# Weight sums kept in DRAM, transposes in other PSUM banks and 512-column value products in a four-layer hybrid network

## The chip, the cores and the metric

The kernel runs on one core of one Trainium2 chip. The metric is the device time of one execution in microseconds, from its first to its last instruction with what the device adds around them; the median of the runs is quoted.

## The reference

`x` is [4, 512, 256] in f32. Four layers are applied, each as `x = x + layer(layernorm(x))`: full attention (16 heads of 128), a gated linear layer, a low-rank attention, and the gated layer again with the same weights. The change touches only the first layer and the norms:

```
q = einsum('bpd,hde->bphe', x, W_Q) + b_Q          # k and v the same with W_K, W_V
scores = einsum('bqhe,bkhe->bhqk', q, k) / sqrt(128), causal
z = einsum('bkhe,bhqk->bqhe', v, softmax(scores))
out = einsum('bqhe,hed->bqd', z, W_O) + b_O
```

The weights do not depend on the batch, so each of the four batches projects with the same ones.

## The kernel before, in words

`attention_full` runs 64 units (4 batches of 16 heads), one per call of `step(i)`, for i = 0 to 64. The order of instructions on each engine is the order in which the code issues them (a manual schedule), and each engine works through its own list without overtaking. Step i holds several units at different ages:

- scores, softmax and `divide` of unit i: four score matmuls of 128 to 512 columns (L468), a masked maximum on VectorE (L476), exponentials on ScalarE (L479), a reciprocal (L491) and the division on GpSimd (L494);
- `turn` of unit i-1 in four pieces (32x32 transposes on VectorE, L503) and `carry(i-1)`: SyncE writes the result to DRAM (`way`, L514), waits for it, and reads it back in four pieces as `probsT` (L517);
- `mix(i-2)`: probabilities times values (L530) and the output products (L552) of a group of four units;
- the query and key projections of unit i+1, and a part of the value projection of the next group.

**The projections are made with seven products instead of eight.** Query and key of a head are taken together as one product of 2x2 blocks; weights and positions are combined first, then seven block products (L395) give the four blocks. `combine_weights` makes three sums s1, s2, s4 and overwrites one block (a21) with a difference: four GpSimd instructions (L306 to L309), of 128 columns for a head (`combine_head`) and of 256 for a group's values (`combine_values`). `combine_positions` makes the like for the positions of a batch (L296 to L299), on GpSimd for batches 1 to 3. The returned list `a11, a12, s4, a22, s1, s2, a21` is indexed by the product's number less one: product 1 uses a11, 2 uses a12, 6 uses s2, 7 uses a21, 5 uses s1, 3 uses s4. In the page the sums are called `extra` (even heads) and `extra_w` (odd heads), the sums of positions `extra_x`.

The order inside `step(i)` matters for all that follows. Product 1 of unit i+1 stands first, then scores 0 and 1, the first `turn`, products 2 and 6, score 2, one value product, product 7, score 3, `divide`, the last turns, `carry(i-1)`, products 5 and 4, `load(i)`, `mix(i-2)`, product 3, `combine_head(i+2)`, and outputs. Between them stand pieces of other layers (`beside`, from a table written by hand).

The sums of unit i+2 are made in step i, and product 6 of step i+1 is the first to read them. SyncE issues every DMA: in a step `way`, four `probsT`, then `load(i)`: for odd i the weights wk and wq of a later pair of heads (L253), for i = 2 mod 4 the values' weights wv (L258), for i = 0 mod 4 the output weights wo (L263).

PSUM has eight banks of 512 columns: three `ps_sc`, two `ps_tp`, two `ps_mm`, one `ps_pz`. Query and key products and the transposes of the norms (L223) and of the gated layer (L1041) use `ps_tp`. A group's value projection (`project_group`) is done in two rounds of seven products of 256 columns, one position tile each time, accumulated in `ps_sc` and `ps_mm` and copied out by ScalarE (L410) and VectorE (L406).

Of the kernel before, what the change touches and what calls it, by code (L numbers as in the profile page):

```python
# [11 lines left out]
F32 = mybir.dt.float32  # L12
# [11 lines left out]
H = 16  # L24
# [42 lines left out]
def network(ctx: ExitStack, tc: tile.TileContext, ins: dict, out: bass.AP):  # L67
# [22 lines left out]

    def ps_pz():
        return psum.tile([P, 512], F32, tag="pz", name="ps_pz")


    ctx.enter_context(tc.manual_schedule())
# [91 lines left out]
    def norm(b, take, extra=None, tiles=range(NT), xT=None, short=False):  # L187


        stats = lnpool.tile([P, NT, 6], F32, name="stats")  # L190
        mv = lnpool.tile([P, NT, 2], F32, name="mv")
        for t in tiles:
            nc.vector.bn_stats(stats[:, t, :], x[b][t])
            nc.vector.bn_aggr(mv[:, t, :], stats[:, t, :])
            yield
        rstd = lnpool.tile([P, NT], F32, name="rstd")
        shift = lnpool.tile([P, NT], F32, name="shift")
        some = slice(tiles[0], tiles[-1] + 1)
        nc.gpsimd.tensor_scalar(rstd[:, some], mv[:, some, 1], EPS, None, ALU.add)
        nc.gpsimd.tensor_tensor(rstd[:, some], rstd[:, some], minus_half[:, some], ALU.pow)  # L200
        if not short:
            nc.gpsimd.tensor_tensor(shift[:, some], mv[:, some, 0], rstd[:, some], ALU.mult)
            nc.gpsimd.tensor_scalar(shift[:, some], shift[:, some], -1.0, 1.0, ALU.mult, ALU.mult)
        yield
        yield
        xT = xT or new_xT()

        def normalise(t):
            xn = lnpool.tile([P, D], F32, name="xn")
            if short:  # L210
                nc.vector.tensor_scalar(
                    xn, x[b][t], mv[:, t, 0:1], rstd[:, t : t + 1], ALU.subtract, ALU.mult
                )
            else:
                nc.scalar.activation(
                    xn, x[b][t], AF.Identity, bias=shift[:, t : t + 1], scale=rstd[:, t : t + 1]
                )
            return xn

        def transpose(t, xn):  # L220
            pt = ps_tp()
            for c in range(DC):
                nc.tensor.transpose(pt[:, c * P : (c + 1) * P], xn[:, c * P : (c + 1) * P], ident)  # L223
# [19 lines left out]
    def attention_full(events, prologue):  # L243
# [2 lines left out]
        n = len(units)  # L246
        wq, wk, wv, wo = {}, {}, {}, {}

        def load_pair(p, w):
            h = 2 * p % H  # L250
            name = "wq" if w is wq else "wk"
            w[p] = slot(f"{name}{p % 2}", name).rearrange("p (c n) -> p c n", c=DC)
            nc.sync.dma_start(w[p], ins["a_" + name][:, :, h * DH : (h + 2) * DH])  # L253

        def load_values(g):
            h = HG * g % H
            wv[g] = slot(f"wv{g % 2}", "wv").rearrange("p (c n) -> p c n", c=DC)
            nc.sync.dma_start(wv[g], ins["a_wv"][:, :, h * DH : (h + HG) * DH])  # L258

        def load_output(g):  # L260
            h = HG * g % H
# [29 lines left out]
        def combine_positions(b, engine):  # L291
# [4 lines left out]
            engine.tensor_tensor(t3, b22, b12, ALU.subtract)  # L296
            engine.tensor_tensor(b12, b12, b11, ALU.subtract)
            engine.tensor_tensor(t2, b22, b12, ALU.subtract)
            engine.tensor_tensor(t4, b21, t2, ALU.subtract)  # L299
            moving[b] = b11, b21, b22, t4, b12, t2, t3  # L300

        def combine_weights(a11, a12, a21, a22, place):

            cols = a11.shape[-1]
            s1, s2, s4 = (place[:, i * cols : (i + 1) * cols] for i in range(3))
            nc.gpsimd.tensor_tensor(s1, a21, a22, ALU.add)  # L306
            nc.gpsimd.tensor_tensor(a21, a11, a21, ALU.subtract)
            nc.gpsimd.tensor_tensor(s2, s1, a11, ALU.subtract)
            nc.gpsimd.tensor_tensor(s4, a12, s2, ALU.subtract)  # L309
            return a11, a12, s4, a22, s1, s2, a21  # L310

        def keep(b):
            def take(xT):
                xTs[b] = xT
                if b:
                    combine_positions(b, nc.gpsimd)

            return take

# [53 lines left out]

        stationary, open_sums = {}, {}

        def combine_head(u):

            p, j = divmod(u, 2)
            (a11, a12), (a21, a22) = (
                [w[p][:, c, j * DH : (j + 1) * DH] for c in range(DC)] for w in (wq, wk)  # L380
            )
            place = extra[2] if j else extra[0][:, 3 * S :]
            stationary[u] = combine_weights(a11, a12, a21, a22, place)

        def combine_values(g):

            a11, a21, a12, a22 = (
                wv[g][:, c, i * HD : (i + 1) * HD] for c in range(DC) for i in range(2)
            )
            stationary["v", g] = combine_weights(a11, a12, a21, a22, extra[0][:, g % 2 * 3 * HD :])  # L390

        def product(i, ps, weights, positions, of_values, start):
            a, b = weights[i - 1], positions[i - 1]
            lhsT, rhs = (b, a) if of_values else (a, b)
            nc.tensor.matmul(  # L395
                ps[:, :HS], lhsT=lhsT, rhs=rhs, start=start, stop=True, skip_group_check=True
            )

        def seven(u, places, biases, positions, chain, side):

            of_values = isinstance(u, tuple)
            weights = stationary[u[:2]] if of_values else stationary[u]
            c11, c12, c21, c22 = places

            def onto(ps, place):
                nc.vector.tensor_tensor(place, place, ps[:, :HS], ALU.add)  # L406

            def out(ps, place, bias):
                if bias is None:
                    nc.scalar.copy(place, ps[:, :HS])  # L410
                else:
                    nc.scalar.activation(place, ps[:, :HS], AF.Identity, bias=bias)  # L412

            def on_chain(i, place, bias):
                if i == 1:
                    open_sums[u, "x"] = chain()
                ps = open_sums[u, "x"]
                product(i, ps, weights, positions, of_values, i == 1)
                out(ps, place, bias)

            def on_side(i, place):
                if i != 3:
                    open_sums[u, "z"] = side()
                ps = open_sums[u, "z"]
                product(i, ps, weights, positions, of_values, i != 3)
                onto(ps, place)

            return {
                1: lambda: on_chain(1, c11, biases[0]),
# [8 lines left out]
        def project(u):  # L438
# [6 lines left out]
            return seven(u, places, biases, moving[b], ps_tp, ps_tp)  # L445

        def project_group(g, t):

            b = HG * g // H
            if t == 0:  # L450
                values[g] = slot(f"v{g % 2}", "v").rearrange("p (t n) -> p t n", t=NT)
            places = [
                values[g][:, t + 2 * i, j * HD : (j + 1) * HD] for j in range(2) for i in range(2)
            ]
            positions = [a[:, t * P : (t + 1) * P] for a in moving[b]]
            return seven(("v", g, t), places, (None, None), positions, ps_sc, ps_mm)

        def score(u, t):

# [121 lines left out]
            project_plainly(u, wk)  # L581
        for t in range(2, NT):
            project_values(0, t)
        combine_positions(0, nc.vector)
        take_bias(0)()
        combine_head(2)
        of_group = {}

        def step(i):
            b, h = divmod(i, H)  # L590
# [148 lines left out]
    def gated(layer, l, xT, xT_before, half, after, last=False):  # L739
# [298 lines left out]
        pt = ps_tp()[:, : nt * DC * P]  # L1038
        for i in range(nt):
            for c in range(DC):  # L1040
                nc.tensor.transpose(  # L1041
# [126 lines left out]
    def attention_lowrank(xTs, events):  # L1168
# [254 lines left out]
        def prologue(i):  # L1423
# [8 lines left out]
            elif stage == -2:  # L1432
                load_keys()
            elif stage == 0:
                buffers()
                probs_of(0, [split(f"squares{k}", k) for k in range(2)])
                probs_of(3, [slot("probs1", "probs3")])
# [291 lines left out]
```

## Time and profile before

| what | value |
|---|---|
| three runs | 1380.65, 1383.38, 1385.46 us (median 1383.38) |
| profiled execution, own time | 1385.7 us |
| its span, first to last instruction | 1383.8 us |
| mean granted TensorE clock | 0.982 |
| TensorE matmul busy | 1286.0 us (93%) |
| VectorE, ScalarE, GpSimd busy | 856.4, 690.2, 729.6 us |
| full attention, first score to last L552 | about 27 to 835 us |
| batches 2 and 3 of it | about 387 to 800 us |

A busy engine need not be at its peak, and a share over the whole span mixes four layers. The chain of waits and the timeline of one step tell what sets the end. In the timeline a row reads: start, duration, engine, line, operation, output<-inputs, shape, count, and in brackets the idle time before it with what ended it. "SPq" is SyncE issuing a DMA; a PE row of "x2" is one f32 matmul, which the profile records as two passes.

### The profile page before, as it was taken

Reading aid. Unit: us, or ns where it says so; the run is one execution under the profiler, and the core shown is the slowest. Engines: PE = TensorE matmul, PEld = TensorE weight load, DVE = VectorE, ACT = ScalarE, POOL = GpSimd, SP = SyncE. Lnnn points to the kernel's source line nnn. Section 1 sums busy time; section 2 is a strip of 40 time slices with the busy share of each in tenths; the row PEclk is TensorE's granted clock in tenths of the full one; section 3 lists DMA queues with packets and bytes.
Section 4 is the critical chain, followed back from the end, with each engine's and each line's share of the span. In section 5 each row is a group of like instructions: output and inputs, shape, how many; then the busy total and the mean of one; then the engine's idle time right before and its main releaser. Section 6 shows DMA issues by size and latency. Waiting matters only on the chain.

```text
span 1383.8 us, 19620 instructions
## 1 busy us (share of the span) xinstructions
PE 1286.0 (93%) x5774; PEld 899.4 (65%) x5774; DVE 856.4 (62%) x2614; ACT 690.2 (50%) x1960; POOL 729.6 (53%) x1433
## 2 busy tenths in 40 slices
PE   8899999999998999899989888998999999999996
PEld 5677776777776777677767565545655676655554
DVE  4566555664775665775746855695566655575756
ACT  3534444454443444343444336655666665767641
POOL 4544443652448344573436655676564765765660
PEclk9999999999999999999999999999999999999998
DMA  3667775555555353454643530000000000000000
GB/s 95 209 202 215 224 196 193 160 160 156 154 166 149 118 160 126 141 164 129 181 117 111 150 107 16 1 1 1 1 1 9 9 9 1 9 1 8 1 9 16
DMA packets 88154, 133.97 MB, mean 97 GB/s; under 512 B 16112, under 2 KB 69872, under 8 KB 88048
## 3 DMA queue, kind: packets, MB, share of 16 engines
q1 hardware_dynamic: 88048, 132.72, 32.3%
q8 instruction: 47, 0.77, 0.2%
q14 instruction: 59, 0.48, 0.1%
HBM read 86.29 MB, written 46.40 MB: 96 GB/s over the span
## 4 chain that ended last, share of the span: by engine, by line
PE 69%; DVE 12%; POOL 8%; ACT 5%; issue 3%; DMA 2%; SPq 1%; DVEq 0%; POOLq 0%; ACTq 0%
PE ps_tp L395 10%; PE ps_sc L468 8%; PE ps_pz L530 8%; PE ps_mm L552 7%; PE ps_mm L781 6%; PE ps_sc L1339 6%; PE ps_tp L1375 4%; PE ps_pz L1395 4%; PE ps_sc L395 3%; PE ps_mm L1413 3%; PE ps_mm L960 2%; PE ps_mm L395 2%; PE ps_mm L1313 1%; POOL probs L1367 1%; DMA probsT<-way 1%
## 5 line engine op out<-in xcount | busy, mean ns | idle before, releaser
L494 POOL TENSOR_SCALAR probs<-probs,sums 128x128 f32<-128x128 f32 (+3 forms) x256 | 137.0, 553 | 368.2 <-DVE sums L491 363.1
L479 ACT ACTIVATE probs<-ps_sc,sums 128x128 f32<-128x128 f32 (+3 forms) x256 | 134.7, 527 | 129.5 <-DVE sums L476 124.9
L468 PE MATMUL ps_sc<-kT,qT 128*128 128x128 f32 (+3 forms) x512 | 172.4, 440 | 10.3 <-ACT probs L479 10.3
L1367 POOL TENSOR_SCALAR probs<-probs,sums 128x160 f32<-128x160 f32 (+3 forms) x224 | 120.4, 555 | 108.4 <-DVE sums L1364 84.8
L476 DVE CUSTOM_DVE_ANT_0 ps_sc<-ps_sc,mask_a 128x128 f32<-128x128 f32 (+3 forms) x256 | 126.8, 500 | 81.2 <-PE ps_sc L468 65.2
L1347 DVE CUSTOM_DVE_ANT_0 ps_sc<-ps_sc,mask_b 128x96 f32<-128x96 f32 (+15 forms) x256 | 112.0, 448 | 94.2 <-PE ps_sc L1339 81.3
L1350 ACT ACTIVATE probs<-ps_sc,sums 128x160 f32<-128x160 f32 (+3 forms) x224 | 114.1, 512 | 99.7 <-DVE sums L1347 78.0
L412 ACT ACTIVATE qT<-ps_tp,bias 128x256 f32<-128x256 f32 x124 | 58.2, 469 | 209.9 <-PE ps_tp L395 209.9
L1339 PE MATMUL ps_sc<-kTb,qTb 128*128 128x32 f32 (+15 forms) x512 | 156.2, 414 | 5.5 <-ACT probs L1350 5.4
L530 PE MATMUL ps_pz<-probsT,v 128*128 128x512 f32 (+3 forms) x512 | 149.2, 434 | 7.0 <-DMA probsT<-way 6.1
L530 PEld LDWEIGHTS ps_pz<-probsT,v 128*128 128x128 f32 x512 | 96.4, 190 | 64.9 <-issue 35.7
L552 PE MATMUL ps_mm<-wo,zT 128*128 128x256 f32 x512 | 123.7, 386 | 1.4 <-ACT qTb L1247 1.3
L503 DVE STREAM_TRANSPOSE squares<-probs 128x512 f32<-128x512 f32 (+3 forms) x256 | 120.6, 491 | 0.0
L1380 ACT COPY probsT<-ps_tp 128x512 f32<-128x512 f32 x160 | 92.2, 585 | 40.5 <-PE ps_tp L1375 39.0
L552 PEld LDWEIGHTS ps_mm<-wo,zT 128*128 128x128 f32 x512 | 97.7, 193 | 17.1 <-ACT qTb L1247 1.7
L1375 PEld LDWEIGHTS ps_tp<-ident,probs 128*128 128x128 f32 x608 | 71.6, 143 | 51.5 <-issue 27.8
L468 PEld LDWEIGHTS ps_sc<-kT,qT 128*128 128x128 f32 x512 | 86.8, 193 | 25.5 <-ACT probs L479 13.9
L1375 PE MATMUL ps_tp<-ident,probs 128*128 128x128 f32 x608 | 96.5, 283 | 4.7 <-ACT xT L225 1.5
L1339 PEld LDWEIGHTS ps_sc<-kTb,qTb 128*128 128x128 f32 x512 | 82.5, 196 | 24.4 <-ACT probs L1350 9.9
L781 PE MATMUL ps_mm<-w_in,cx 128*128 128x512 f32 (+1 forms) x256 | 91.7, 496 | 2.6 <-DVE cx L766 1.1
L543 DVE TENSOR_SCALAR zT<-ps_pz,bias 128x512 f32<-128x512 f32 x64 | 47.9, 748 | 66.9 <-PE ps_pz L530 66.9
L395 PE MATMUL ps_tp<-extra_x,wk 128*128 128x256 f32 x248 | 75.4, 386 | 3.6 <-ACT qT L412 3.5
(215 smaller groups left out, 2616.5 us busy)
## 6 DMA issues: line engine op xcount, KB each, us to landing
way<-squares SPq DMA_DIRECT2D x64, 640.0 KB, 2.9
probsT<-way SPq DMA_DIRECT2D x256, 160.0 KB, 3.3
wv<-in_a_wv_dram SPq DMA_DIRECT2D x16, 512.0 KB, 5.1
wq<-in_a_wq_dram SPq DMA_DIRECT2D x32, 256.0 KB, 4.0
wk<-in_a_wk_dram SPq DMA_DIRECT2D x32, 256.0 KB, 3.9
wo<-in_a_wo_dram SPq DMA_DIRECT2D x16, 512.0 KB, 4.7
x<-in_x_dram SPq DMA_DIRECT2D x16, 128.0 KB, 3.8
out_dram<-x SPq DMA_DIRECT2D x16, 128.0 KB, 1.7
```

The lines of the kernel that those rows point to most:

```text
L395: nc.tensor.matmul(ps[:, :HS], lhsT=lhsT, rhs=rhs, start=start, stop=True, skip_group_check=True)
L468: nc.tensor.matmul(ps[:, :m], lhsT=queries[u][:, t * P : (t + 1) * P], rhs=keys[u][:, :m], start=True, stop=True,)
L476: nc.vector.tensor_tensor_reduce(ps[:, :m], ps[:, :m], mask[:, S - m :], -scale, 3.0e38, ALU.add, ALU.min, nmax[:, t : t + 1])
L479: nc.scalar.activation(pr[:, t, :m], ps[:, :m], AF.Exp, bias=nmax[:, t : t + 1], scale=-1.0, accum_out=total[:, t : t + 1],)
L494: nc.gpsimd.tensor_scalar(pr[:, t, :m], pr[:, t, :m], inv[:, t : t + 1], 1.0, ALU.mult, ALU.mult)
L503: nc.vector.transpose(squares[u].rearrange("p (j n b) -> p n j b", j=NQ, b=Q)[:, f : f + m], probs[u][0][:, k:, k * P : (k + 1) * P].rearr ...
L530: nc.tensor.matmul(z[:, :, k:, :], lhsT=v[:, k, j * DH : (j + 1) * DH], rhs=pT[:, :, f : f + m, :], start=(k == 0), stop=(k == NT - 1),)
L552: nc.tensor.matmul(po[:, :D], lhsT=zTs[HG * g + i][:, t].rearrange("p i b -> p (i b)"), rhs=wo[g][:, i, :], start=(i == 0), stop=(i == HG ...
L781: nc.tensor.matmul(ps[:, : hi - lo], lhsT=cx[:, c, i * P : (i + 1) * P], rhs=w_in[:, c, lo:hi], start=(c == 0), stop=(c == DC - 1),)
L1339: nc.tensor.matmul(ps, lhsT=q[:, t % 2 * 4 + i].rearrange("p h q -> p (h q)"), rhs=kT[:, :m], start=True, stop=True,)
L1367: nc.gpsimd.tensor_scalar(probs[i][:, :m], probs[i][:, :m], inv[:, i : i + 1], 1.0, ALU.mult, ALU.mult)
L1375: nc.tensor.transpose(pt.rearrange("p (h i q) -> p h i q", h=4, i=4)[:, :, i, :], lw["probs"][t][s][i][:, k * P : (k + 1) * P], ident,)
```

## The change

Four edits.

1. **Weight sums kept.** From batch 1 on, the sums of each head and group and the overwritten wk and wv are stored to DRAM (`keep_head`, `keep_values`). In batches 2 and 3 `combine_head` and `combine_values` issue a load from there in place of the four GpSimd instructions, and wk and wv are loaded as they were stored.
2. **Positions.** `combine_positions` is done on VectorE for every batch, in steps 8 and 9 of the batch before, two instructions each.
3. **Transposes** of the norms and of the gated layer use `ps_mm` during full attention, and `ps_tp` afterwards.
4. **Values.** A group's value projection is one round over four steps; each product is two matmuls of 256 columns into the two halves of a bank, and one copy of 512 columns.

In the first batch `combine_head(2)` is also issued ahead of the addition of the output bias. The core of the diff:

```
+        kept = {}
+        def keep_or_load(what, place):
+            if what not in kept:
+                kept[what] = dram.tile([P, place.shape[-1]], F32, name="kept_%s%d" % what)
+                nc.sync.dma_start(kept[what], place)
+            else:
+                nc.sync.dma_start(place, kept[what])
...
-            w[p] = slot(f"{name}{p % 2}", name).rearrange("p (c n) -> p c n", c=DC)
-            nc.sync.dma_start(w[p], ins["a_" + name][:, :, h * DH : (h + 2) * DH])
+            flat = slot(f"{name}{p % 2}", name)
+            w[p] = flat.rearrange("p (c n) -> p c n", c=DC)
+            if w is wk and ("k", h) in kept:
+                keep_or_load(("k", h), flat)
+            else:
+                nc.sync.dma_start(w[p], ins["a_" + name][:, :, h * DH : (h + 2) * DH])
...
-            nc.gpsimd.tensor_tensor(s1, a21, a22, ALU.add)
-            nc.gpsimd.tensor_tensor(a21, a11, a21, ALU.subtract)
-            nc.gpsimd.tensor_tensor(s2, s1, a11, ALU.subtract)
-            nc.gpsimd.tensor_tensor(s4, a12, s2, ALU.subtract)
+            if not known:
+                nc.gpsimd.tensor_tensor(s1, a21, a22, ALU.add)
+                nc.gpsimd.tensor_tensor(a21, a11, a21, ALU.subtract)
+                nc.gpsimd.tensor_tensor(s2, s1, a11, ALU.subtract)
+                nc.gpsimd.tensor_tensor(s4, a12, s2, ALU.subtract)
...
-            place = extra[2] if j else extra[0][:, 3 * S :]
-            stationary[u] = combine_weights(a11, a12, a21, a22, place)
+            known = ("h", u % H) in kept
+            if known:
+                keep_or_load(("h", u % H), extra_of_head(u))
+            stationary[u] = combine_weights(a11, a12, a21, a22, extra_of_head(u), known)
+
+        def keep_head(u):
+            if u >= H and ("h", u % H) not in kept:
+                keep_or_load(("h", u % H), extra_of_head(u))
+            if u >= H and u % 2 and ("k", u % H - 1) not in kept:
+                keep_or_load(("k", u % H - 1), wk[u // 2].rearrange("p c n -> p (c n)"))
...
-            pt = ps_tp()
+            pt = for_transposes[0]()
...
+            def products(w, i):
+                return [(t, moving[b][i][:, t * P : (t + 1) * P], w) for t in range(2)]
+            return seven(("v", g), stationary["v", g], places, (None, None), products, ps_sc, ps_mm)
...
-                if j % 2 == 0:
-                    of_group.update(project_group(g + 1, j // 2))
-                group = [(1,), (2, 6), (), ()] if j % 2 == 0 else [(7,), (5,), (4,), (3,)]
+                if j == 0:
+                    of_group.update(project_group(g + 1))
+                group = [
+                    [(1,), (), (2,), ()],
+                    [(6,), (), (), ()],
+                    [(7,), (5,), (), ()],
+                    [(4,), (3,), (), ()],
+                ][j]
...
+            if b + 1 < B and 8 <= h < 10:
+                next(of_positions.setdefault(b + 1, combine_positions(b + 1)))
...
             of_head(5, 4)
+            if 2 <= i + 1 < n:
+                keep_head(i + 1)
+            if i % HG == 1 and i // HG + 1 < groups:
+                keep_values(i // HG + 1)
             load(i)
```

`combine_values` and `keep_values` are the same for a group's sums ("e", 768 columns) and wv ("v", 1024 columns). In the built order the list of SyncE grows from 529 to 601 instructions: 32 stores (16 of a head's sums, 8 of a pair's wk, 4 and 4 for the values) and 40 loads of sums (32 of a head, 8 of a group) are added, and 24 loads of wk and wv change their source. A head's sums are 128 x 384 f32, 192 KB.

More of the change, by code (lines that the diff above doesn't have):

```diff
@@ L92, in ps_pz @@
         return psum.tile([P, 512], F32, tag="pz", name="ps_pz")
+    for_transposes = [ps_mm]
     ctx.enter_context(tc.manual_schedule())
@@ L251, in load_pair @@
             name = "wq" if w is wq else "wk"
-            w[p] = slot(f"{name}{p % 2}", name).rearrange("p (c n) -> p c n", c=DC)
-            nc.sync.dma_start(w[p], ins["a_" + name][:, :, h * DH : (h + 2) * DH])
+            flat = slot(f"{name}{p % 2}", name)
[4 more added lines that the diff above has]
+                nc.sync.dma_start(w[p], ins["a_" + name][:, :, h * DH : (h + 2) * DH])
         def load_values(g):
             h = HG * g % H
-            wv[g] = slot(f"wv{g % 2}", "wv").rearrange("p (c n) -> p c n", c=DC)
-            nc.sync.dma_start(wv[g], ins["a_wv"][:, :, h * DH : (h + HG) * DH])
+            flat = slot(f"wv{g % 2}", "wv")
+            wv[g] = flat.rearrange("p (c n) -> p c n", c=DC)
+            if ("v", h) in kept:
+                keep_or_load(("v", h), flat)
+            else:
+                nc.sync.dma_start(wv[g], ins["a_wv"][:, :, h * DH : (h + HG) * DH])
         def load_output(g):
@@ L289, in attention_full, with combine_positions @@
         HS, HD = S // 2, HG // 2 * DH
-        def combine_positions(b, engine):
+        def combine_positions(b):
             b11, b12, b21, b22 = (xTs[b][:, c, i * HS : (i + 1) * HS] for c in range(DC) for i in range(2))
@@ L295, in combine_positions, with combine_weights @@
             t2, t3, t4 = (of_batch[:, i * HS : (i + 1) * HS] for i in range(3))
[L296 to L299, printed above, removed]
             moving[b] = b11, b21, b22, t4, b12, t2, t3
-        def combine_weights(a11, a12, a21, a22, place):
+            nc.vector.tensor_tensor(t3, b22, b12, ALU.subtract)
+            nc.vector.tensor_tensor(b12, b12, b11, ALU.subtract)
+            yield
+            nc.vector.tensor_tensor(t2, b22, b12, ALU.subtract)
+            nc.vector.tensor_tensor(t4, b21, t2, ALU.subtract)
+            yield
+        def combine_weights(a11, a12, a21, a22, place, known):
             cols = a11.shape[-1]
             s1, s2, s4 = (place[:, i * cols : (i + 1) * cols] for i in range(3))
-            nc.gpsimd.tensor_tensor(s1, a21, a22, ALU.add)
-            nc.gpsimd.tensor_tensor(a21, a11, a21, ALU.subtract)
-            nc.gpsimd.tensor_tensor(s2, s1, a11, ALU.subtract)
-            nc.gpsimd.tensor_tensor(s4, a12, s2, ALU.subtract)
+            if not known:
[3 more added lines that the diff above has]
+                nc.gpsimd.tensor_tensor(s4, a12, s2, ALU.subtract)
             return a11, a12, s4, a22, s1, s2, a21
@@ L314, in take @@
                 xTs[b] = xT
-                if b:
-                    combine_positions(b, nc.gpsimd)
             return take
@@ L374, in attention_full, with extra_of_head, extra_of_group @@
         stationary, open_sums = {}, {}
+        def extra_of_head(u):
+            return (extra[2] if u % 2 else extra[0][:, 3 * S :])[:, : 3 * DH]
+        def extra_of_group(g):
+            return extra[0][:, g % 2 * 3 * HD :][:, : 3 * HD]
         def combine_head(u):
@@ L389, in combine_values, with keep_values, seven, multiply @@
             )
[L390 to L402, printed above, removed]
-            c11, c12, c21, c22 = places
[L405 to L412, printed above, removed]
+            known = ("e", HG * g % H) in kept
+            if known:
+                keep_or_load(("e", HG * g % H), extra_of_group(g))
+            stationary["v", g] = combine_weights(a11, a12, a21, a22, extra_of_group(g), known)
+        def keep_values(g):
+            if HG * g >= H and ("e", HG * g % H) not in kept:
+                keep_or_load(("e", HG * g % H), extra_of_group(g))
+                keep_or_load(("v", HG * g % H), wv[g].rearrange("p c n -> p (c n)"))
+        def seven(u, weights, places, biases, products, chain, side):
+            c11, c12, c21, c22 = places
+            def multiply(i, ps, start):
+                for at, lhsT, rhs in products(weights[i - 1], i - 1):
+                    nc.tensor.matmul(
+                        ps[:, at * HS : (at + 1) * HS],
+                        lhsT=lhsT,
+                        rhs=rhs,
+                        start=start and at == 0,
+                        stop=True,
+                        skip_group_check=True,
+                    )
+            def like(ps, place):
+                cols = math.prod(place.shape[1:])
+                ps = ps[:, :cols]
+                return ps if len(place.shape) == 2 else ps.rearrange("p (t n) -> p t n", t=place.shape[1])
             def on_chain(i, place, bias):
@@ L417, in on_chain @@
                 ps = open_sums[u, "x"]
-                product(i, ps, weights, positions, of_values, i == 1)
-                out(ps, place, bias)
+                multiply(i, ps, i == 1)
+                if bias is None:
+                    nc.scalar.copy(place, like(ps, place))
+                else:
+                    nc.scalar.activation(place, like(ps, place), AF.Identity, bias=bias)
             def on_side(i, place):
@@ L424, in on_side @@
                 ps = open_sums[u, "z"]
-                product(i, ps, weights, positions, of_values, i != 3)
-                onto(ps, place)
+                multiply(i, ps, i != 3)
+                nc.vector.tensor_tensor(place, place, like(ps, place), ALU.add)
             return {
@@ L444, in project, with project_group, products @@
             biases = [bias[:, i, h : h + 1] for i in range(2)]
-            return seven(u, places, biases, moving[b], ps_tp, ps_tp)
-        def project_group(g, t):
+            def products(w, i):
+                return [(0, w, moving[b][i])]
+            return seven(u, stationary[u], places, biases, products, ps_tp, ps_tp)
+        def project_group(g):
             b = HG * g // H
-            if t == 0:
-                values[g] = slot(f"v{g % 2}", "v").rearrange("p (t n) -> p t n", t=NT)
+            values[g] = slot(f"v{g % 2}", "v").rearrange("p (t n) -> p t n", t=NT)
             places = [
-                values[g][:, t + 2 * i, j * HD : (j + 1) * HD] for j in range(2) for i in range(2)
+                values[g][:, 2 * i : 2 * i + 2, j * HD : (j + 1) * HD] for j in range(2) for i in range(2)
             ]
-            positions = [a[:, t * P : (t + 1) * P] for a in moving[b]]
-            return seven(("v", g, t), places, (None, None), positions, ps_sc, ps_mm)
+            def products(w, i):
+                return [(t, moving[b][i][:, t * P : (t + 1) * P], w) for t in range(2)]
+            return seven(("v", g), stationary["v", g], places, (None, None), products, ps_sc, ps_mm)
         def score(u, t):
@@ L583, in attention_full @@
             project_values(0, t)
-        combine_positions(0, nc.vector)
+        run(combine_positions(0))
+        combine_head(2)
         take_bias(0)()
-        combine_head(2)
-        of_group = {}
+        of_group, of_positions = {}, {}
         def step(i):
@@ L1037, in gated @@
         oT = wide("w1", half, "oT", nt * DV).rearrange("p (t n) -> p t n", t=nt)
-        pt = ps_tp()[:, : nt * DC * P]
+        pt = for_transposes[0]()[:, : nt * DC * P]
         for i in range(nt):
@@ L1434, in prologue @@
             elif stage == 0:
+                for_transposes[0] = ps_tp
                 buffers()
```

## The prediction

> **What bounds the kernel now.** First the page's shares.
>
> ```profile
> PE 1286.0 (93%) x5774; PEld 899.4 (65%) x5774; DVE 856.4 (62%) x2614; ACT 690.2 (50%) x1960; POOL 729.6 (53%) x1433
> ```
>
> TensorE is busy 93% of the span, GpSimd 53%. The change takes work from GpSimd, ScalarE and VectorE and leaves the number of matmuls as it is. So it can gain only where TensorE waits. I therefore asked for TensorE's waits in the stretch that holds batches 2 and 3 (377 to 788 us; matmuls busy 384.0 of 411 us).
>
> ```profile
> PE ps_sc L468 <- ACT probs L479: 9.6, 5, 2.8
> PE ps_tp L395 <- POOL extra_w L308: 3.3, 2, 1.8
> PE ps_tp L223 <- DVE qT L406: 2.4, 6, 0.5
> ```
>
> Columns: total us, times, longest. The sums cost TensorE 3.3 us, in two places; the norms' transposes, waiting for a bank, 2.4. There is little to win: all of TensorE's idle time there is 27 us.
>
> Then the timeline of two plain steps, 54 and 55, TensorE and the DMA queue (and GpSimd for the sums).
>
> ```profile
> 668.42 0.59 PE L395 MATMUL ps_tp<-extra_x,extra_w 128*128 128x256 f32 x2
> 670.36 1.02 PE L468 MATMUL ps_sc<-kT,qT 128*128 128x512 f32 x2
> 673.86 0.35 SPq L514 DMA_DIRECT2D way<-squares  x1
> 675.42 0.45 POOL L306 TENSOR_TENSOR extra<-wk 128x128 f32<-128x128 f32 x1
> 676.90 0.46 POOL L309 TENSOR_TENSOR extra<-wq,extra 128x128 f32<-128x128 f32 x1
> 676.87 1.73 SPq L517 DMA_DIRECT2D probsT<-way  x4
> 678.64 0.55 SPq L258 DMA_DIRECT2D wv<-in_a_wv_dram  x1
> 678.78 0.59 PE L395 MATMUL ps_tp<-extra_x,extra 128*128 128x256 f32 x2
> ```
>
> The reader should see a race. Product 6 of step 54 (668.42) and of step 55 (678.78) are 10.36 us apart. GpSimd makes the sums for the second from 675.42 to 677.36, 1.4 us ahead of it. SyncE is done with the reads of `probsT` and the load of step 54 only at 679.19, after that product has begun.
>
> **1. The loads of a head's sums (32, issued in steps 30 to 61).** By the built order such a load stands behind `way`, four `probsT` and the step's loads, and product 6 of the next step waits for it. TensorE does not overtake, so score 2, score 3 and everything behind them wait too. Score 3 leads to the exponential, the reciprocal, the last turns and `way`: the next load of sums hangs on the late product, so the delay comes back every step and no slack is carried over. The loop, in step 54:
>
> - product 6 to `way`: 673.86 - 668.42 = 5.44 us. The new order puts two value matmuls in front of score 3 where one stood: one more at 0.43 us (spacing of products, 671.65 to 672.08). 5.87.
> - `way` to the first `probsT`: 676.87 - 673.86 = 3.01.
> - `probsT` and wv: 679.19 - 676.87 = 2.32, and 0.1 to the next issue.
> - issue to landing of 192 KB: the trace has no such load. The nearest is wk, 256 KB, median 3.9; I take 3.9. Bounds: 2.5, the fastest `probsT` piece (160 KB), and 5.0, wv (512 KB), in case the sums queue behind it.
> - landing to matmul 0.1 (the L530 that waited began 0.04 to 0.14 after the landing).
>
> ```profile
> DMA to landing us min/median/max: 2.5/3.3/5.5
> wk<-in_a_wk_dram SPq DMA_DIRECT2D x15, 256.0 KB, 3.9
> wv<-in_a_wv_dram SPq DMA_DIRECT2D x7, 512.0 KB, 5.0
> ```
>
> (The first line is that of `probsT`, min/median/max; the others end with the median.) Sum 15.3 us, where TensorE needs 10.36: 4.9 us late. In odd steps wk and wq stand ahead, 1.3 us of issue in place of 0.65: step 55 gives 16.0 against 10.79, 5.2 late. I read the same points for all 32 steps (distance of product 6 to the next; product 6 to the end of the last load):
>
> - 20 steps, nearly all of 10.4 to 12.8 us: 4.5 to 5.8 late, 101 us;
> - 7 with more work of other layers (steps 34, 35, 40, 49, 56, 57, 61): 1.9 to 4.0 late, 20 us;
> - 5 (36, 37, 42, 50, 58), mostly of 15 to 19 us: 1 us together.
>
> **122 us**; with 2.5 for the landing it is 84, with 5.0 it is 155. From this I take 6 off, since a waiting TensorE lets ScalarE catch up and the 9.6 us of L468 above lie in these steps (bounds 0 and 10).
>
> The Trainium skill, "DMA: Bandwidth & Descriptors", section "Anatomy of one DMA — SWDGE (gpsimd) path", fits a DMA as about 2.0 us plus bytes/436e3, which for 192 KB gives an estimate of 2.45 us; by it the sum would be about 82 us. That fit is for another queue, and the row of wk here says 3.9 where it would say 2.6.
>
> **2. The clock.** Each wait also costs clock. The windows around a wait of 2.72 us before score 2 in step 47:
>
> ```profile
> 580.50:583.93 3.43, 0.71 (x3) 0.47 (x3) 2.49 (x8) 1.11 (x5) 0.91 (x1) 1.00 0.79 211
> 583.93:587.34 3.41, 3.41 (x7) 2.04 (x7) 1.11 (x4) 2.00 (x6) 0.00 (x0) 0.50 0.02 6
> ```
>
> First pair of numbers is TensorE's busy time, the third from the end the granted clock: after a window of 3.41 us with 2.7 idle, the next runs at 0.50. The half-clock periods of the trace all begin on one grid of 3.41 us; each window that was idle for 1.97 us or more was followed by one (9 of 9), and matmuls of 256 columns then issue every 427 ns in place of 216. A wait of 4 to 5 us always leaves one window idle for 2 us. Half of 3.41 is 1.7 us lost; part of a period may fall inside the wait, where it is free: I take 1.4. It falls on the 3 us between product 6 and score 3, thus into the loop. 26 steps are over 2 us late: 26 x 1.4 = **36 us** (bounds 0 and 26 x 1.7 = 44).
>
> The Trainium skill, "TensorE: Matmul & The Clock Gate", section "HAM oscillation — how this bites in real kernels", warns of idle gaps above about 3.4 us and shows a kernel that starts each tile cold after a DMA wait, so it speaks against this change. By its threshold the 20 long waits alone would count, 28 us; the trace shows 2 us to be enough.
>
> **3. What is removed.** GpSimd loses 128 instructions at 0.47 (heads), 32 at 0.75 (groups) and 12 at 0.73 (positions): 93 of 729.6 us. It waits 363 us for the reciprocals (L494), so only TensorE's 3.3 us were paid for, and they lie in steps that now wait for the load. 0; at best -3. The 12 position instructions on VectorE (0.39 each, row L406), two in each of six steps, sit before score 3's maximum, for which VectorE waits 0.8 us in step 55. 0; without that cover 4.7.
>
> **4. Stores in batch 1 (32) and loads of group sums (8).** A store's issue, 0.4 to 0.6 us, stands between `probsT` and `load(i)`. wk and wq land about 4 us after issue (step 53: 668.83, hence 672.7) and GpSimd reads them from 675.42: 2.7 us of slack against at most 1.1 to 1.7 of added issue. 0. The stores' traffic can slow `probsT`: in the first 200 us, the stretch of most traffic, L530 waited 4.1 us for it: 0 to +4. Group sums are first read a step later than the head's that stand before them: 0.
>
> **5. Banks and wide copies.** Copies: 120 x 0.365 become 60 of about 0.585 (row L1380) on ScalarE, 90 x 0.39 become 45 of about 0.75 (row L543) on VectorE: both less, neither on the path. Side products now hold one of the two `ps_mm` banks for a whole step in four; the transposes and outputs there share the other. Gain at best the transposes' bank waits before 845 us, some 5; loss at worst a copy of 0.42 for each of some 30 transposed tiles, 13. I take 0: in batches 2 and 3 the waits of part 1 cover it. Starting `combine_head(2)` first: 0, at best -0.6.
>
> **Sum.** 122 - 6 + 36 = +152 on the profiled execution's 1385.7 us (span 1383.8): 1538. The median of the runs lies 2.3 us lower, so the forecast is 1535.
>
> **Rivals.**
>
> *A. The loads land sooner, and little clock is lost.* Landing 2.5 and no half clock: 1383 + 84 - 6, about 1461; with either one alone, 1497 (half clock, short landing) or 1499 (no half clock). For: a quieter DMA queue, since steps get longer. Against: no wk landed under 3.4 us, and every grid window idle for 2 us drew a half-clock period.
>
> *B. Worse.* The sums queue behind wv and wo (5.0 us and more) and each late step loses 1.7: 155 + 44 = 199, 1582. For: all go through one queue. Against: wq, right behind wk, lands as fast as wk.
>
> *C. Faster.* The load is no bound because SyncE reaches it early, and only the relief remains: 3.3 us of sums, 5 of transposes, part of the 9.6 of L468: about -12, 1371. Decided at one place, product 6: the load must land within the step. In 20 steps SyncE gets to it only when that product is due or later, so even a landing at once would be no gain. It needs the load to be issued ahead of `probsT`, which the built order denies.
>
> *D. The change does not do what it says.* Were nothing kept, time would stay; but the order shows the 72 additional DMAs, and product 6 waiting for a DMA.
>
> **Chances.** Forecast (waits and half clock, 1500 to 1575) 0.70; A 0.17; B 0.08; C 0.03; no change 0.02. About 0.3% is what a measurement of this kernel can tell from no change. Slower 0.95, same 0.02, faster 0.03. The range of 8 in 10 takes in A and B as worked out: 1461 to 1585.
>
> **What would show it.** Right: product 6 waiting for DMA `extra` some 29 times, near 5 us each, 120 us together; steps 31 to 62 at 15 to 17 us; granted clock of 0.8 to 0.95 in the slices of batches 2 and 3; batches 0 and 1 and the last 540 us within 5 us of before. Wrong: `probsT` or `way` waiting in place of product 6, a full clock there, or long waits for `ps_mm` in the first half.

## The result, and the profile after

The changed kernel takes **1569.13 us** (median of 4 runs, 1566.17 to 1570.69), the kernel before 1382.02 beside it (4 runs, 1378.47 to 1385.46): a ratio of 1.135, 95% interval 1.132 to 1.139. The forecast was 1535, with 1461 to 1585 as range. The page of the changed kernel (its lines have other numbers: L395 is now L441, L468 L518, L514 L564, L517 L567), busy shares, granted clock in tenths by slice, and the chain that ended last:

```profile
PE 1346.5 (86%) x5774; PEld 937.3 (60%) x5774; DVE 851.9 (54%) x2581; ACT 695.7 (44%) x1900; POOL 639.1 (41%) x1261
...
PEclk9999999999888989888988998989999999999998
...
PE 57%; DMA 15%; DVE 10%; SPq 5%; ACT 5%; POOL 4%; issue 3%; DVEq 0%; POOLq 0%; ACTq 0%
```

GpSimd did lose 90 us of work (729.6 to 639.1) and the matmuls are as many as before, 5774. But DMA, 2% of the chain before, is 15% now, the clock is below 9 tenths in many slices of batches 2 and 3, and the matmuls' busy time grew by 60 us: the same work at a lower clock. The waits, whole span (total us, times, longest):

```profile
PE ps_tp L441 <- DMA extra_w<-kept_h: 76.0, 16, 6.2
PE ps_tp L441 <- DMA extra<-kept_h: 64.8, 13, 7.1
```

TensorE waits 140.8 us for the loads of a head's sums, 29 times, 4.9 us each. The kernel before waited 3.3 us for these sums. Where the time came, by stretches (product 6 of step 30 and of step 62 are the cuts). The first line is the kernel before, the second the changed one; after the bounds and the length: busy time of TensorE, of its weight loads, VectorE, ScalarE, GpSimd, then granted clock, DMA share and GB/s:

```profile
367.00:777.00 410.00, 386.10 (x1589) 287.25 (x1588) 267.97 (x787) 176.46 (x522) 208.08 (x425) 0.99 0.49 145
```

```profile
375.00:963.00 588.00, 438.99 (x1589) 319.20 (x1587) 266.22 (x775) 182.76 (x494) 126.68 (x266) 0.88 0.39 119
```

The same 1589 matmul records, 410 us before and 588 after: **178 of the span's 184.5 us lie in these 32 steps.** The first stretch grew from 367 to 375 us, the last shrank from 606.5 to 605.1. In the 32 steps TensorE's idle time went from 24 to 149 us (+125), and the half-clock periods from 10 to 147 us, of which 36 lie inside waits; the other 111 cost half their length, 55 us against 5 before (+50). 125 and 50 make 175 of the 178. (Idle time and periods are added up from the trace: TensorE's records and the granted clock between the two products.)

The loop that the forecast described, as the timeline shows it for steps 54 and 55:

```profile
815.88 0.97 PE L441 MATMUL ps_tp<-extra_x,extra_w 128*128 128x256 f32 x2 [5.10 <-DMA extra_w<-kept_h]
816.64 1.48 PE L518 MATMUL ps_sc<-kT,qT 128*128 128x384 f32 x2
...
820.01 1.02 PE L518 MATMUL ps_sc<-kT,qT 128*128 128x512 f32 x2
...
833.99 1.19 PE L441 MATMUL ps_tp<-extra_x,extra 128*128 128x256 f32 x2 [5.39 <-DMA extra<-kept_h]
```

```profile
823.51 0.32 SPq L564 DMA_DIRECT2D way<-squares  x1
826.49 1.74 SPq L567 DMA_DIRECT2D probsT<-way  x4
828.27 0.43 SPq L259 DMA_DIRECT2D wv<-kept_v  x1
828.80 0.38 SPq L259 DMA_DIRECT2D extra<-kept_h  x1
```

Product 6 (815.88), 7.6 us to `way` (823.51), 3.0 to the reads of `probsT`, 2.3 to the load of the sums, 5.05 to its landing at 833.85, and product 6 of the next step at 833.99: 18.1 us, where the kernel before needed 10.36. The load is the only thing in the last 5.4 us. Score 2 (816.64) takes 1.48 us where it took 0.81: the clock. Two windows around the wait that ends at 815.88 show it; the first pair of numbers after the length is TensorE's busy time, the third number from the end the granted clock:

```profile
812.60:816.10 3.50, 0.22 (x1) 0.25 (x2) 0.00 (x0) 0.00 (x0) 0.00 (x0) 1.00 0.66 200
816.10:819.50 3.40, 3.40 (x8) 2.33 (x8) 1.34 (x4) 1.15 (x3) 0.00 (x0) 0.50 0.02 5
```

### The profile page after: what moved, and what is told of

The parts are those of the page before. It is cut to its first block, busy times and chain, and to the rows that moved or that the text cites. A ratio compares the mean times of both kernels' runs of the same rounds, so it can differ in the third digit from the quotient of the medians.

```text
span 1568.3 us, 19305 instructions
## 1 busy us (share of the span) xinstructions
PE 1346.5 (86%) x5774; PEld 937.3 (60%) x5774; DVE 851.9 (54%) x2581; ACT 695.7 (44%) x1900; POOL 639.1 (41%) x1261
## 4 chain that ended last, share of the span: by engine, by line
PE 57%; DMA 15%; DVE 10%; SPq 5%; ACT 5%; POOL 4%; issue 3%; DVEq 0%; POOLq 0%; ACTq 0%
PE ps_tp L441 9%; PE ps_sc L518 7%; PE ps_mm L842 5%; PE ps_pz L580 5%; DMA way<-squares 5%; PE ps_sc L1400 5%; PE ps_mm L602 5%; DMA extra<-kept_h 4%; DMA extra_w<-kept_h 4%; PE ps_sc L441 4%; PE ps_tp L1436 3%; PE ps_pz L1456 3%; SPq L567 3%; PE ps_mm L1474 2%; ACT probs L529 2%
## 5 line engine op out<-in xcount | busy, mean ns | idle before, releaser
L518 PE MATMUL ps_sc<-kT,qT 128*128 128x128 f32 (+3 forms) x512 | 191.0, 479 | 1.8 <-ACT probs L529 1.8
L602 PE MATMUL ps_mm<-wo,zT 128*128 128x256 f32 x512 | 127.4, 395 | 5.6 <-ACT xT L227 3.7
L518 PEld LDWEIGHTS ps_sc<-kT,qT 128*128 128x128 f32 x512 | 97.1, 212 | 19.9 <-ACT probs L529 3.8
L1400 PEld LDWEIGHTS ps_sc<-kTb,qTb 128*128 128x128 f32 x512 | 83.7, 198 | 24.3 <-ACT probs L1411 10.2
L441 PE MATMUL ps_tp<-extra_x,extra_w 128*128 128x256 f32 x62 | 26.7, 521 | 77.3 <-DMA extra_w<-kept_h 76.0
L441 PE MATMUL ps_tp<-extra_x,wk 128*128 128x256 f32 x248 | 80.1, 407 | 2.5 <-ACT qT L463 1.7
```

Of the source, the lines that this page charges most:

```text
L441: nc.tensor.matmul(ps[:, at * HS : (at + 1) * HS], lhsT=lhsT, rhs=rhs, start=start and at == 0, stop=True, skip_group_check=True,)
L518: nc.tensor.matmul(ps[:, :m], lhsT=queries[u][:, t * P : (t + 1) * P], rhs=keys[u][:, :m], start=True, stop=True,)
L602: nc.tensor.matmul(po[:, :D], lhsT=zTs[HG * g + i][:, t].rearrange("p i b -> p (i b)"), rhs=wo[g][:, i, :], start=(i == 0), stop=(i == HG ...
L1400: nc.tensor.matmul(ps, lhsT=q[:, t % 2 * 4 + i].rearrange("p h q -> p (h q)"), rhs=kT[:, :m], start=True, stop=True,)
```

## The experiments

Theory: the load of a head's sums is issued behind `way` and `probsT`, lands after product 6 wants it, and hangs on the product 6 of the step before; half clock follows each wait. Rivals: the other three edits, the added DMA traffic, or something that builds up.

**e1, nothing kept.** The stores and with them the loads are left out:

```
         def keep_head(u):
+            return
...
         def keep_values(g):
+            return
```

> The changed kernel with nothing kept: no stores, and GpSimd makes the sums in every batch; the positions on VectorE, the transposes in the other banks and the wide value products stay. Theory (the loss is the load of a head's sums, which SyncE issues too late for product 6): the steps 30 to 61 go back to about 400 us, no wait of product 6 over 2 us, total 1380 to 1395 us; the 8 us that the first 375 us became longer stay if they come from the other three edits, and go if they come from the stores. Rival (a good part of the 187 us is from the banks, the wide products or the positions): over 1410 us.

Measured: 1384.89 us (10 runs), ratio 0.9987, interval 0.9968 to 1.0005. The 32 steps:

```profile
376.50:784.10 407.60, 387.07 (x1590) 288.26 (x1588) 266.03 (x767) 175.60 (x490) 205.77 (x421) 0.99 0.50 147
```

So without the kept sums the other three edits together neither bring nor cost anything that this can tell, and there is no loss (beside late loads they make it some 20 us larger, see e5). The first stretch stays long, 376.5 us, so the stores are not its cause.

**e2, the load issued earlier.** All four edits, one move:

```
+        def fetch_head(u):
+            if u < n and ("h", u % H) in kept:
+                keep_or_load(("h", u % H), extra_of_head(u))
...
             known = ("h", u % H) in kept
-            if known:
-                keep_or_load(("h", u % H), extra_of_head(u))
...
+            fetch_head(i + 2)
             of_head(1)
             if now:
                 score(i, 0)
```

> The changed kernel with one move: the load of the sums of head i+2 is issued at the start of step i, ahead of way and probsT, in place of behind them; everything else is kept, the same DMAs and the same bytes. Theory: the load lands some 10 us before product 6 wants it, the loop through DRAM is cut, granted clock above 0.97 in batches 2 and 3, 1375 to 1395 us in total. Rival (more DMA traffic or the source of the loads is what costs): hardly better than 1569 us, or waits of mix for probsT in place of those of product 6, above 1420 us.

Measured: 1377.33 us, ratio 0.9951 (0.9921 to 0.9980). The 32 steps and the clock by slice:

```profile
375.00:768.80 393.80, 379.63 (x1590) 285.32 (x1588) 263.46 (x767) 175.46 (x490) 126.86 (x266) 1.00 0.58 177
```

```profile
PEclk9999999999999999999999998999999999999998
```

The same DMAs and bytes as in the changed kernel, at a higher rate (177 GB/s), and 194 us less in these steps. **The place of the load in SyncE's list is the cause, not the traffic.** The expectation put the landing some 10 us ahead of need; it is less, 3.4 us at the least and 6.5 in the median of the 32 steps, since the load still stands behind the loads of the step before.

**e3, the sums ahead of the weights.** The load stays behind `probsT` but stands ahead of `load(i)`:

```
+            fetch_head(i + 2)
             load(i)
```

> The load of a head's sums stands ahead of the step's loads of weights (wk and wq, wv, or wo), still behind probsT. It saves 0.65 us of issue in even and 1.3 in odd steps, and no longer queues behind their data: landing near 3.5 to 3.9 us in place of 4.1 and 5.2. Theory (every us on the loop is paid in each late step): 27 steps times about 1.8 us, and a little of the clock, 1500 to 1530 us. Rival (the wait is for something other than this load): within 10 us of 1569.

Measured: 1504.91 us, 64 less. Issue and landing of the sums, the changed kernel first (KB each, median us to landing), then e3 with its waits:

```profile
extra<-kept_h SPq DMA_DIRECT2D x16, 192.0 KB, 5.2
extra_w<-kept_h SPq DMA_DIRECT2D x16, 192.0 KB, 4.1
```

```profile
extra<-kept_h SPq DMA_DIRECT2D x16, 192.0 KB, 3.8
extra_w<-kept_h SPq DMA_DIRECT2D x16, 192.0 KB, 3.6
```

```profile
PE ps_tp L443 <- DMA extra_w<-kept_h: 53.2, 15, 5.0
PE ps_tp L443 <- DMA extra<-kept_h: 40.7, 12, 4.5
```

The sums do queue behind the data of the loads ahead of them: 0.5 us behind wk and wq, 1.4 behind wv or wo. With the issue saved (0.65 and 1.3) that is 1.9 us for each of 27 waits, 51 us. In the 32 steps TensorE's idle time fell by 48 us (149 to 102) and the half-clock periods from 147 to 89 us, 17 us less lost; together that is the gain. Every microsecond on the loop is paid in each late step. Even here the load is not alone: the four `probsT`, 640 KB, are issued just ahead of it.

**e4, the wait filled.** Ten matmuls whose result nobody reads, ahead of product 6 in 27 steps:

```
-            of_head(2, 6)
+            of_head(2)
+            if 31 <= i <= 62 and i not in (37, 38, 43, 51, 59):
+                ps = ps_pz()
+                a = moving[b][0]
+                for _ in range(10):
+                    nc.tensor.matmul(ps[:, :HS], lhsT=a[:, :P], rhs=a, start=True, stop=True)
+            of_head(6)
```

> The changed kernel with ten more matmuls of 256 columns (4.3 us, their result is not used) ahead of product 6 in the 27 steps that wait, to keep TensorE busy while it would wait. Theory (half clock after each wait is a term of its own, about 2 us in each late step, since it lengthens product 6 to way from 5.9 to 7.8): granted clock over 0.97, product 6 to way back at 5.9 us, total 1505 to 1535 us although work is added. Rival (the clock costs nothing because it falls into the waits): 1569 us or more.

Measured: 1521.95 us. The 32 steps:

```profile
378.30:920.60 542.30, 503.32 (x2130) 389.63 (x2129) 266.04 (x775) 180.05 (x494) 126.78 (x266) 0.99 0.42 129
```

540 matmul records more (27 steps, ten matmuls, two passes), and 46 us less than the changed kernel: clock 0.99 where it was 0.88. From product 6 to `way` it is 6.24 us in the mean of steps 31 to 61, against 7.84. **The half clock is a term of its own, 46 us.** What is left over the kernel before, 132 us, is wait and filler.

**e5, the first edit alone**, on the kernel before (the diff is the part on kept sums).

> The kernel before with the first edit alone: the weight sums kept and loaded as in the changed kernel, with positions, transposes and value products as before. Theory (the loads alone make the loss): product 6 waits for the load some 28 times; one value matmul less stands in front of score 3 (0.43 us), so each late step is 0.43 shorter: 1545 to 1570 us. Rival (the other three edits are needed for the loss): under 1500 us.

Measured: 1549.72 us, ratio 1.1185 (1.1117 to 1.1252), as the theory has it; 28 waits of product 6, 131.1 us. The 20 us less than with all four edits are in part the value product that no longer stands ahead of score 3 (28 x 0.43 = 12 us) and in part the first stretch (368.1 in place of 375.0 us).

**e6, the first edit alone, loaded early.** e5 with the move of e2.

> The kernel before with the first edit alone, and the load of a head's sums issued at the start of the step. It tells what the kept sums are worth without the other edits. Theory (the sums on GpSimd cost TensorE some 3 us, and a less loaded GpSimd little more): 1376 to 1384 us, no more than 8 under the kernel before. Rival (the gain of 7 us seen with the early loads comes from the other three edits): within 2 us of the kernel before.

Measured: **1368.92 us**, ratio 0.9883 (0.9836 to 0.9930), the fastest kernel of this study. It is better than the theory had it, by 7 us. Its 32 steps:

```profile
366.20:762.50 396.30, 380.69 (x1589) 284.76 (x1588) 267.46 (x787) 176.62 (x522) 129.56 (x270) 1.00 0.58 175
```

Against 410 us before: TensorE's idle time fell from 23.9 to 15.7 us (the waits of score 2 for the exponentials from 9.6 to 4.5, those for the sums from 3.6 to none), and with the longest of these waits the three half-clock periods went too, 10.2 us, another 5.

```profile
PE ps_sc L511 <- ACT probs L522: 4.5, 3, 1.7
```

Why waits for exponentials go with GpSimd's sums is seen in the kernel before, step 47. The sums stand on GpSimd ahead of a piece of another layer (`part`); VectorE waits for that piece, the maximum and the exponential stand behind it, and score 2 waits 2.72 us:

```profile
579.93 0.46 POOL L309 TENSOR_TENSOR extra<-wq,extra 128x128 f32<-128x128 f32 x1
580.35 1.06 POOL L950 TENSOR_TENSOR part<-kv,a 128x512 f32<-128x512 f32 x1
581.44 0.69 DVE L979 TENSOR_TENSOR o<-o,part 128x512 f32<-128x512 f32 x1 [2.30 <-POOL part L950]
583.33 1.10 PE L468 MATMUL ps_sc<-kT,qT 128*128 128x384 f32 x2 [2.72 <-ACT probs L479]
```

In e6 the wait at this place is 1.43 us. The longest wait of the kernel before, 2.77 us in step 57, has a like chain behind it (`cx` of another layer in place of `part`), and e6 has none there.

**e7, e9, e10, the other edits beside early loads.** e7 is e2 with the transposes back in `ps_tp`; e9 is e6 with the positions on VectorE; e10 is e7 with the positions on GpSimd, so e6 with the wide value products.

> All four edits with the early loads, but the transposes of the norms back in the banks of the query and key products. It tells what the other banks cost or bring in the first 375 us, which were 8 us longer in the changed kernel. If the shared bank is the cause: the first 375 us shorter by 3 to 8 us and 1370 to 1375 us in total. If chance in the half-clock periods is: within 3 us of 1377, the waits for the transposes' copies going from one bank to the other.

> Kept sums loaded at the start of the step (the kernel of 1369 us), and the positions' sums on VectorE in steps 8 and 9 of the batch before. It tells the price of that edit by itself. Theory (12 instructions moved, each hidden): within 3 us of 1369. Rival (the 5 us between 1369 and the 1374 with three edits come from it): 1372 to 1375 us.

> Kept sums loaded at the start of the step, and the value products of 512 columns; positions on GpSimd and transposes in the old banks. It tells the price of the wide products by themselves. Theory (fewer copies, off the path, but one value product more ahead of score 3, which makes the way through DRAM 0.43 us later): 1370 to 1376 us. Rival (fewer copies bring time): under 1367 us.

Measured: e7 1374.02 (ratio 0.9912, 0.9881 to 0.9943), e9 1371.36 (0.9898, 0.9868 to 0.9928), e10 1376.73 (0.9932, 0.9904 to 0.9960). All are faster than before and none than e6. e9 lies within the 3 us that its theory allowed, e10 0.7 us above the range of its own; the first stretch of e7 is 6.1 us shorter than that of e2 (368.9 against 375.0), as its first case had it, but its total fits both cases. The intervals overlap, so a price of a few us for any one of the three edits is not settled. What the traces, one execution of each kernel, show of the first stretch, up to product 6 of step 30: 366.2 to 372.6 us in the five kernels with the old banks (e5, e6, e7, e9, e10), 370.5 to 378.3 in the six with the other ones (the changed kernel, e1 to e4, e8). With the other banks its half-clock periods add up to 6.8 to 20.5 us, with the old ones, e10 apart, to 3.4 to 6.8. How such a period arises is seen in the changed kernel, two windows and TensorE's timeline:

```profile
256.30:259.70 3.40, 0.89 (x5) 0.47 (x6) 1.22 (x4) 1.36 (x3) 3.19 (x6) 1.00 0.52 143
259.70:263.10 3.40, 2.94 (x8) 2.10 (x9) 0.00 (x0) 0.37 (x1) 3.32 (x6) 0.51 1.03 288
```

```profile
257.25 0.41 PE L225 MATMUL ps_mm<-ident,xn 128*128 128x128 f32 x2 [0.95 <-DVE xT L227]
258.62 0.44 PE L225 MATMUL ps_mm<-ident,xn 128*128 128x128 f32 x2 [0.96 <-ACT xn L217]
259.67 0.61 PE L225 MATMUL ps_mm<-ident,xn 128*128 128x128 f32 x2 [0.61 <-DVE xT L227]
```

Three waits of the norm's transposes, for copies out of the one free bank and for the normalised tile, fall into one window; it is idle for 2.5 us, and the next runs at half clock. e10 has the old banks and a long first stretch too (372.6 us, 13.7 us of half clock), so the banks are not the only way to it.

**e8, every second load early.** Odd heads' sums at the start of the step, even ones as in the changed kernel:

```
-            if known:
+            if known and u % 2 == 0:
...
+            if i % 2 and i + 2 < n and ("h", (i + 2) % H) in kept:
+                keep_or_load(("h", (i + 2) % H), extra_of_head(i + 2))
             of_head(1)
```

> The changed kernel with the loads of odd heads issued at the start of the step and those of even heads left where they are (late, behind wv or wo). Theory (each late step pays for itself, about 6 us of wait and clock, since no slack is carried from step to step): the late half of 16 heads pays its part, 80 to 110 us, 1460 to 1490 us in total. Rival (the loss builds up because one late step makes the next one late): with every second step free the loop is cut and the total is under 1430 us.

Measured: 1472.52 us.

```profile
PE ps_tp L441 <- DMA extra<-kept_h: 69.4, 14, 7.3
```

14 waits of 5.0 us, as long as before, and half of the loss: 95 us over e2, where all loads late cost 192. Each late step pays for itself; nothing builds up from step to step, and a step without a wait in between does not help.

## Why the prediction was right, and which terms were off

The direction and the mechanism were right; the size was 152 us forecast on the profiled execution and 184.5 measured. The 32 us between them are, as read below, some 20 of landing less 8 of relief, 14 of clock, and 8 in the first stretch that were put at nothing, less 1 in the last.

**1. The loads.** The loop is as worked out: in the plain steps 30 and 59, which have no wait before them, product 6 to `way` takes 5.87 us in the changed kernel, the 5.44 and 0.43 of the forecast; `way` to `probsT` is 2.95 to 3.0 us in nearly all. 29 waits came where 29 were counted, 27 of them over 2 us where 26 were; and the five steps for which the forecast had next to no wait have 0 to 1.7 us each. The term that was mis-sized is the landing: 3.9 was taken; it is 4.1 behind wk and wq and 5.2 behind wv and wo, 0.7 more in the mean, some 20 us. The row of wq, which lands as fast behind wk as wk alone, was read as "no queueing"; e3 shows the queueing. The upper bound of 5.0 had it. The relief from a waiting TensorE was taken as 6; e4, whose mean of 6.24 us from product 6 to `way` stands against 6.26 + 0.43 of the kernel before, puts it near 14.

**2. The clock.** 36 forecast, bounds 0 and 44; 46 by e4, 50 by the length of the periods, both over the upper bound. The number was right, 26 periods in the 32 steps; their length was not. 18 of them are two windows long: after the wait of 5.39 us in step 55 the clock is at half for 6.8 us. So they cost 55 us, 2.1 each and not 1.4; 5 of it was there before. The threshold of about 3.4 us of idle that the prediction cites from the Trainium skill ("TensorE: Matmul & The Clock Gate", section "HAM oscillation — how this bites in real kernels") is not what these traces show: 2.72 us inside one window drew a half-clock period in the kernel before (step 47), while 3.52 us that fall into two windows, ahead of product 6 of step 57 at 872.33, drew none:

```profile
867.31:870.72 3.41, 1.50 (x8) 0.99 (x7) 2.14 (x7) 1.50 (x5) 0.00 (x0) 1.00 1.00 275
870.72:874.13 3.41, 1.80 (x8) 1.44 (x9) 0.45 (x1) 0.47 (x1) 0.00 (x0) 1.00 0.30 118
874.13:877.55 3.42, 3.42 (x15) 2.66 (x14) 2.72 (x8) 2.64 (x7) 0.00 (x0) 1.00 0.00 0
```

**3. GpSimd's relief at 0 to -3.** In the changed kernel it is hidden, as said. Uncovered (e6) it is worth some 14 us in the 32 steps (16 by the medians), more than the -12 of rival C, which counted the transposes and not the half-clock periods that go with the waits. The step that failed is "only TensorE's 3.3 us were paid for": the sums also held up other layers' work on GpSimd, and through VectorE and ScalarE the scores (e6, step 47).

**4. Stores at 0.** Right: e5 has all of them and its first stretch is 368.1 us, against 367.0.

**5. Banks and wide copies at 0.** Right for the sum of the three other edits (e1: 0.9987), but not as worked out: in the changed kernel the first stretch grew by 7.9 us, 5 of them by half-clock periods (13.7 us in place of 3.4). "Batches 0 and 1 within 5 us" was missed.

Rival A is out: no load of the changed kernel landed under 3.8 us, and the clock was lost. Rival B had the queueing and the larger clock term right; its 199 us were nearer than the forecast's 152. Rival C named the condition under which the change would gain, a load issued ahead of `probsT`; e2 and e6 are that kernel, and they gain, 6.5 and 16 us by the medians. The fit of a DMA as 2.0 us plus bytes/436e3 that the prediction cites from the Trainium skill ("DMA: Bandwidth & Descriptors", section "Anatomy of one DMA — SWDGE (gpsimd) path"; 2.45 us for these sums) is too low for every load of the changed kernel, all of which stand behind other DMAs. It is near those few of e2 and e6 that had the queue almost to themselves: 2.39 and 2.35 us for the first load of each, issued 2.6 us or more behind wq, 2.74 and 2.75 in step 59, ahead of which no weights were loaded. What the sum lacked was the queue.

## What to carry to other kernels

Before work of an idle engine is replaced by a load, find the place of that load in its queue and the first instruction that reads it. A load behind a DMA that waits for this step's result is a poor prefetch for the next step: it closes a loop, and where the loop (15 to 16 us here, worked out ahead) is longer than the step (10.4 to 12.8 us), the loop sets the step, of which the transfer is only a part. Moved ahead of that DMA, the same load with the same bytes turned a loss of 13.5% into a gain of 0.5%, and of 1.2% with the first edit alone.

## What the runs showed of the hardware that was not expected

- A load of 192 KB landed in 2.35 to 2.75 us the four times that little was in flight ahead of it (e2, e6), 3.6 to 3.8 us in the median behind four `probsT` reads of 160 KB (e3), 4.1 behind these and two loads of 256 KB, 5.2 behind these and one of 512 KB: what is ahead in the queue adds about as much again as the load takes by itself.
- A wait costs more than its length: 29 waits of 4.9 us brought 137 us more of half-clock time (36 us of it inside waits), and ten unused matmuls per step (116 us of work in all, 503.3 us of busy time less the 387 of the other matmuls at full clock) made the kernel 47 us faster.
- Short waits close together do the same as one long one: three waits of 0.6 to 0.96 us of single transposes left a window 2.5 us idle and cost a half-clock period. And a long one split by the edge of a window can do nothing: 3.52 us as 1.9 and 1.6 us left the clock at 1.00.
